# Row norms of a Mamba and attention kernel, computed in two halves of their rows

## The chip, the cores and the metric

The kernel runs on one core of a Trainium2 chip. The metric is the device time of one execution in microseconds. Three runs of the kernel before took 3666.76, 3668.60 and 3671.24 us; their median is 3668.6 us.

A core has engines that each work through their own fixed list of instructions, in order: TensorE (PE, matmuls and transposes; PEld is its weight load), VectorE (DVE), ScalarE (ACT), GpSimd (POOL) and SyncE (SP, which here only issues DMAs). An instruction waits on semaphores for results of other engines, and everything behind it on its engine waits with it. POOL issues some DMAs too, in the same list as its arithmetic.

## The reference, cut to what matters

Eight sequences of 512 tokens with 256 features go through a Mamba layer and then a layer of attention with gated experts and a feed-forward network. Everything is float32.

```python
x = x + _layernorm(mamba(_layernorm(x)))
x = x + _layernorm(moe_layer(_layernorm(x)))

def _layernorm(x, axis=-1, eps=1e-05):
    m = jnp.mean(x, axis=axis, keepdims=True)
    v = jnp.var(x, axis=axis, keepdims=True)
    return (x - m) / jnp.sqrt(v + eps)

def moe_layer(src):
    src = _ln(src + _moe_attn(src), ln1_g, ln1_b)
    return _ln(src + relu(src @ W1 + b1) @ W2 + b2, ln2_g, ln2_b)
```

Each sequence so meets six row norms: before Mamba, after it, before the attention layer, the two inside (`_ln`, with a gain and an offset behind), and one after. Mamba contains a scan over the 512 tokens for 512 channels and 16 states. The attention has 16 heads of width 64; values and outputs pass through 8 experts per head, of which a gate keeps two.

## The kernel before

**Tiling.** A sequence (here "batch" b, 0 to 7) is held either as rows, tokens on 128 partitions, 4 tiles of 128 tokens with 256 features each, or as features on partitions with the 512 tokens along the free dimension. Transposes on PE (`to_features`, L285 to L291) turn one into the other.

**Stages of a batch.** `front(b)` (L305) loads the rows (`xin`), norms them to `xn_m`, transposes (`ps_tr_m`), projects (`ps_in`), runs the convolution on DVE (`xs`) and prepares the step sizes (`ln`, `u`). `mamba(b)` (L500) runs the scan: 32 steps of three DVE instructions each, a product `h<-bt,dtx`, a scan `h<-da,h` and a product `h<-h,ct`, all 128x1024; the two states of a step are summed into `xc` by accumulating DMAs, which POOL issues (L574). Then come the output projection (`ps_out`), the norm of `x`, the residual sum, the norm to `xn`, its transposes (`ps_tr_g`), the gate scores (`ps_sel`) and the gate's selection on DVE (`key`, `hit`, `s`, `top`). Attention goes through 8 pairs of heads (`Pair`, L797): queries and keys `ps_qk`, which are rotated by `sin` and `qk` on DVE and four accumulating DMAs issued by POOL (L841); scores `ps_s`, their maximum `low` (DVE), exponentials (ACT), transposes `ps_pt`, values `ps_v`, weighted by the gate into `ve` (DVE) and added up by three instructions on POOL (L932 to L934) into `v`; the product `ps_o`; the gated `og` (DVE) and the output sums `ps_a`. `feed_forward(b)` (L1026) follows beside the next batch's attention, with the norms of `y` and two of `z`. The last batch's feed-forward network is `last_net` (L1121), in two halves of 256 tokens, whose norms of `y_last` have two row tiles instead of four.

**A norm.** `_Norm.__call__` (L74) is a generator. For each row tile it issues two DVE instructions, the sums (`bn_stats`, into `ln_st`) and their aggregate (`bn_aggr`, mean and variance into `ln_mv`). Then one DVE instruction adds epsilon to the variances of all tiles (`tensor_scalar`, into `ln_rs`), one POOL instruction takes them to the power of -0.5 (L85, in place in `ln_rs`), and for each tile one DVE instruction applies it: subtract the mean, multiply by `ln_rs`. All DVE instructions pass through the wrapper `_Vector`, so they all have line 175 in the profile. There are 51 norms: 45 of four row tiles and 6 of two.

**What sets the order.** The kernel writes out the order of each engine's instructions itself (`manual_schedule`), from a planner (`_Order`, L98). PE's work carries planned durations (`pe`), DVE's too (`_Vector`: 0.02 us, later 0.09 more, and 1.12 ns a column). Attention is the main line; fronts, Mamba layers, feed-forward networks and gates are generators that run beside it. What a generator yields is the planned time until its next part is due, counted from the end of its last DVE instruction in the plan:

```python
        r[0] = max(self.here, self.vec if self.vec > vec else 0.0) + wait
```

A part is put into the order when it is due and the planned DVE has room (`run`, L145); of several that are due, the one of lowest rank goes first. So a yielded number decides which other instructions stand between two parts of a norm in DVE's list, and how early the transposes behind the norm stand in PE's. It makes no engine wait on the chip. In `last_net` the norm's parts are run one after the other with no regard to the yields (`normed`, L1166).

Of the kernel before, what the change touches and what calls it, by code (L numbers as in the profile page):

```python
# [28 lines left out]
ALU = mybir.AluOpType  # L29
# [13 lines left out]
EPS = 1e-5  # L43
# [22 lines left out]
class _Norm:  # L66
# [7 lines left out]
    def __call__(self, out, rows):  # L74

        nc, vector, n = self.nc, self.vector, len(rows)
        st = self.pool.tile([P, n, 6], F32, tag="ln_st", name="ln_st")
        mv = self.pool.tile([P, n, 2], F32, tag="ln_mv", name="ln_mv")
        rs = self.pool.tile([P, n], F32, tag="ln_rs", name="ln_rs")
        for i, r in enumerate(rows):  # L80
            vector.bn_stats(st[:, i, :], r)
            vector.bn_aggr(mv[:, i, :], st[:, i, :])
            yield 0.0
        vector.tensor_scalar(rs, mv[:, :, 1], EPS, None, ALU.add)
        nc.gpsimd.tensor_tensor(rs, rs, self.power[:, :n], ALU.pow)  # L85
        yield 1.5
        for i, r in enumerate(rows):
            vector.tensor_scalar(
                out[:, i, :], r, mv[:, i, 0:1], rs[:, i : i + 1], ALU.subtract, ALU.mult
            )  # L90
            yield 0.1
# [1291 lines left out]
```

## Time and profile before

| What | Value |
|---|---|
| Median of three runs | 3668.6 us |
| Profiled execution | 3673.76 us, its span 3672.0 us |
| Mean granted TensorE clock | 0.970 |
| Powers of 128x4 on POOL | 45, 73.1 us busy, 1624 ns mean |
| Powers of 128x2 on POOL | 6, 4.2 us busy, 698 ns mean |
| Aggregates on DVE | 192, 35.0 us busy, 182 ns mean |
| DVE idle before applications, until a power | 53.5 us, 34 times |
| POOL idle before powers, until the TENSOR_SCALAR of `ln_rs` | 161.2 us, 32 times |

The profile is one execution, slower than the median of the runs by 5.2 us. Its page gives busy times, a chain of waits and groups of instructions; the trace behind it answers for single tiles, stages and instructions. An engine's idle time counts only where the engine, or what waits for it, is on the way to the end. Durations of single instructions include the time in which they were held up once started. Successive DVE instructions overlap by some 0.08 us, so four applications of 0.41 us take 1.38 us.

### The profile page before, as it was taken

How to read it: one execution, taken by the hardware profiler on the slowest of the kernel's cores; microseconds unless marked ns; L12 is line 12 of the kernel's file. 1: busy time of each engine (PE TensorE's matmuls, PEld its weight loads, DVE VectorE, ACT ScalarE, POOL GpSimd, SP SyncE). 2: the span in 40 equal slices, each digit the busy share in tenths (PEclk: the TensorE clock that was granted, in tenths of full speed). 3: DMA queues.
4: the chain of work that ended last, by engine and by line, in shares of the span. 5: the costliest groups of instructions: out<-in, count | busy, mean ns of one | idle time of the engine just before them, and what ended most of it. 6: DMA issues, size and time to landing. Idle time of an engine off the chain costs nothing.

```text
span 3672.0 us, 35171 instructions
## 1 busy us (share of the span) xinstructions
PE 3406.9 (93%) x11250; PEld 1678.2 (46%) x11250; DVE 3048.9 (83%) x3198; ACT 1664.0 (45%) x2866; POOL 1677.5 (46%) x1597
## 2 busy tenths in 40 slices
PE   5768989989899999999999999999999999999997
PEld 3533334444344444444444444445444444446555
DVE  7878898799989898999989998899988999654443
ACT  5624443545543455344644446444553444332332
POOL 1425663354645545354454555355443657232321
PEclk8879999999999999999999999999999999999999
DMA  4927774577866768577755868568765778443430
GB/s 136 198 73 175 179 173 115 150 181 176 196 144 165 176 169 195 124 182 181 197 139 143 203 154 204 146 154 188 183 171 128 181 186 203 118 126 92 115 106 26
DMA packets 282534, 574.06 MB, mean 156 GB/s; under 512 B 37224, under 2 KB 124520, under 8 KB 282096
## 3 DMA queue, kind: packets, MB, share of 16 engines
q1 hardware_dynamic: 201584, 422.88, 40.0%
q0 software_dynamic: 80768, 148.95, 24.3%
q8 instruction: 91, 1.49, 0.2%
q14 instruction: 91, 0.75, 0.1%
HBM read 403.36 MB, written 19.42 MB: 115 GB/s over the span
## 4 chain that ended last, share of the span: by engine, by line
PE 48%; DVE 27%; issue 8%; DMA 7%; ACT 5%; POOL 5%; SPq 0%; DVEq 0%; POOLq 0%; ACTq 0%
PE ps_v L916 14%; DVE h L175 11%; PE ps_a L1000 9%; DMA xc<-h 5%; PE ps_qk L819 5%; PE ps_s L857 4%; PE ps_a L1020 3%; PE ps_o L946 3%; PE ps_pt L892 3%; DVE ve L175 2%; DVE og L175 2%; DVE low L175 2%; DVE xs L175 2%; PE ps_in L347 1%; DVE hit L175 1%
## 5 line engine op out<-in xcount | busy, mean ns | idle before, releaser
L916 PE MATMUL ps_v<-wv,xt 128*128 128x512 f32 x2048 | 945.8, 605 | 20.4 <-DVE y L175 13.3
L932 POOL TENSOR_TENSOR ve<-ve 128x512 f32<-128x512 f32 x256 | 423.6, 1655 | 1148.1 <-DVE ve L175 996.5
L1000 PE MATMUL ps_a<-og,wo 128*128 128x512 f32 x1792 | 847.1, 606 | 28.0 <-DVE og L175 27.7
L872 ACT ACTIVATE p<-ps_s,low 128x512 f32<-128x512 f32 x512 | 347.3, 683 | 723.0 <-DVE low L175 722.6
L574 POOL DMA_DIRECT2D xc<-h x504 | 463.8, 1099 | 382.1 <-DMA xc<-h 170.0
L916 PEld LDWEIGHTS ps_v<-wv,xt 128*128 128x128 f32 x2048 | 385.9, 193 | 536.9 <-issue 481.3
L175 DVE TENSOR_TENSOR_SCAN h<-da,h 128x1024 f32<-128x1024 f32 x228 | 541.2, 2374 | 10.3 <-ACT da L511 0.4
L1000 PEld LDWEIGHTS ps_a<-og,wo 128*128 128x128 f32 x1792 | 326.5, 192 | 440.9 <-issue 371.4
L881 ACT ACTIVATE p<-p,total 128x512 f32<-128x512 f32 x512 | 341.5, 714 | 252.2 <-DVE total L175 251.4
L175 DVE TENSOR_TENSOR og<-o,gb 128x1024 f32<-128x1024 f32 x256 | 320.1, 1271 | 128.8 <-ACT o L952 81.6
L175 DVE TENSOR_TENSOR ve<-ps_v,gv 128x1024 f32<-128x1024 f32 x256 | 311.7, 1218 | 130.0 <-PE ps_v L916 102.7
L898 ACT COPY pt<-ps_pt 128x1024 f32<-128x1024 f32 x256 | 256.9, 1005 | 347.3 <-PE ps_pt L892 345.9
L511 ACT ACTIVATE da<-dt,decay 128x511 f32<-128x511 f32 x512 | 339.8, 714 | 103.9 <-DVE h L175 100.8
L175 DVE TENSOR_TENSOR h<-bt,dtx 128x1024 f32<-128x1024 f32 x228 | 321.2, 1409 | 34.6 <-DMA xc<-h 34.4
L175 DVE TENSOR_TENSOR h<-h,ct 128x1024 f32<-128x1024 f32 x256 | 338.0, 1320 | 3.8
L175 DVE TENSOR_REDUCE low<-ps_s 128x2 f32<-128x1024 f32 x256 | 310.8, 1214 | 26.8 <-PE ps_s L857 26.1
L933 POOL TENSOR_TENSOR ve<-ve 128x256 f32<-128x256 f32 x256 | 318.1, 1243 | 20.1
L841 POOL DMA_DIRECT2D qk<-sin x256 | 204.5, 1209 | 256.7 <-DVE qk L175 128.9
L857 PE MATMUL ps_s<-qk 64*128 64x512 f32 x1024 | 295.0, 650 | 24.3 <-ACT p L872 14.0
L892 PEld LDWEIGHTS ps_pt<-ident,p 128*128 128x128 f32 x2048 | 239.4, 141 | 124.1 <-issue 87.1
L946 PE MATMUL ps_o<-pt,v 128*64 128x512 f32 x1024 | 249.9, 615 | 30.8 <-POOL v L934 16.7
L892 PE MATMUL ps_pt<-ident,p 128*128 128x128 f32 x2048 | 266.8, 274 | 6.4 <-ACT pt L898 2.6
(165 smaller groups left out, 3579.0 us busy)
## 6 DMA issues: line engine op xcount, KB each, us to landing
gb<-go_d SPq DMA_DIRECT2D x512, 256.0 KB, 4.8
xc<-h POOLq DMA_DIRECT2D x504, 256.0 KB, 5.6
wv<-in_wv_dram SPq DMA_DIRECT2D x128, 512.0 KB, 5.9
wo<-in_wo_dram SPq DMA_DIRECT2D x504, 128.0 KB, 4.0
ct<-bc_d SPq DMA_DIRECT2D x64, 512.0 KB, 5.8
bt<-bc_d SPq DMA_DIRECT2D x57, 512.0 KB, 5.6
wqk<-in_wqk_dram SPq DMA_DIRECT2D x64, 256.0 KB, 2.7
qk<-sin POOLq DMA_DIRECT2D x256, 64.0 KB, 4.8
```

What stands on the lines that cost most here:

```text
L175: return getattr(self.engine, name)(*args, **kw)
L511: nc.scalar.activation(das[k % 2][:, j, 1:S], dt[:, m, 1:S], AF.Exp, scale=decay[:, m, g + j : g + j + 1],)
L574: nc.gpsimd.dma_start(out=xc[:, k % NC, :], in_=hs[k][:, j, :], accum_op=ALU.add)
L857: nc.tensor.matmul(ps[:, j, :], lhsT=self.qk[feats, 0, bass.ts(t, P)], rhs=self.qk[feats, 1, :], start=True, stop=True,)
L872: nc.scalar.activation(p[:, j, :], ps[:, j, :], AF.Exp, bias=low[:, j : j + 1], accum_out=total[:, j : j + 1],)
L881: nc.scalar.mul(p[:, j, :], p[:, j, :], total[:, j : j + 1])
L892: nc.tensor.transpose(pp[:, j, bass.ts(i, P)], self.p[t][:, j, bass.ts(i, P)], ident)
L916: nc.tensor.matmul(ps[:, i, :], lhsT=self.xt[:, c, bass.ts(t + i, P)], rhs=self.wv[:, c, :], start=(c == 0), stop=(c == ND - 1),)
L932: nc.gpsimd.tensor_tensor(ve[:, :, 0:4], ve[:, :, 0:4], ve[:, :, 4:8], ALU.add)
L933: nc.gpsimd.tensor_tensor(ve[:, :, 0:2], ve[:, :, 0:2], ve[:, :, 2:4], ALU.add)
L946: nc.tensor.matmul(po[j * HP : j * HP + HP, 0, :], lhsT=self.v[:, j, t, :], rhs=self.pt[:, j, t, :], start=(t == 0), stop=(t == NT - 1),)
L1000: nc.tensor.matmul(pa[:, c, :], lhsT=self.wo[:, i, bass.ts(c, P)], rhs=self.og[q][:, i, :], start=(self.pair == 0 and k == 0), stop=(self. ...
```

## The change

A norm goes through its row tiles in two halves. After the sums and aggregates of a half, its own small `tensor_scalar` and its own power on POOL are issued, so there are two of each per norm, on half the columns. The first half's two instructions stand in front of the second half's sums, in the same part of the generator. The second half's follow its last aggregate. Then 0.6 instead of 1.5 is yielded to the planner before the applications, which are as before. A norm of two row tiles becomes two halves of one tile.

```diff
-        for i, r in enumerate(rows):
-            vector.bn_stats(st[:, i, :], r)
-            vector.bn_aggr(mv[:, i, :], st[:, i, :])
-            yield 0.0
-        vector.tensor_scalar(rs, mv[:, :, 1], EPS, None, ALU.add)
-        nc.gpsimd.tensor_tensor(rs, rs, self.power[:, :n], ALU.pow)
-        yield 1.5
+
+        for at in (slice(0, n // 2), slice(n // 2, n)):
+            for i in range(at.start, at.stop):
+                vector.bn_stats(st[:, i, :], rows[i])
+                vector.bn_aggr(mv[:, i, :], st[:, i, :])
+                yield 0.0
+            vector.tensor_scalar(rs[:, at], mv[:, at, 1], EPS, None, ALU.add)
+            nc.gpsimd.tensor_tensor(rs[:, at], rs[:, at], self.power[:, at], ALU.pow)
+        yield 0.6
         for i, r in enumerate(rows):
             vector.tensor_scalar(
                 out[:, i, :], r, mv[:, i, 0:1], rs[:, i : i + 1], ALU.subtract, ALU.mult
```

## The prediction

> **What bounds the kernel.** I read the page's head first, then the busy times by stage, then what TensorE (PE) waited for, then the reciprocal root itself (the tile `ln_rs`), last single norms in order of time.
>
> ```profile
> span 3672.0 us, 35171 instructions
> PE 3406.9 (93%) x11250; PEld 1678.2 (46%) x11250; DVE 3048.9 (83%) x3198; ACT 1664.0 (45%) x2866; POOL 1677.5 (46%) x1597
> PE 48%; DVE 27%; issue 8%; DMA 7%; ACT 5%; POOL 5%; SPq 0%; DVEq 0%; POOLq 0%; ACTq 0%
> ```
>
> PE is busy for 93% of the span, and the change takes no matmul away: all it can win is part of PE's 265 us of idle time. The busy times by stage (length, PE, PEld, DVE, ACT, POOL, then clock, DMA) say where that lies:
>
> ```profile
> 0.00:222.00 222.00, 136.02 (x630) 96.09 (x630) 177.94 (x185) 109.52 (x180) 56.34 (x78) 0.83 0.66 156
> 860.00:1290.00 430.00, 398.78 (x1258) 186.64 (x1256) 388.97 (x387) 203.84 (x343) 221.13 (x202) 0.97 0.72 170
> 1720.00:2150.00 430.00, 413.51 (x1317) 194.22 (x1316) 385.83 (x403) 205.89 (x351) 215.68 (x198) 0.99 0.68 168
> 3651.00:3672.00 21.00, 6.66 (x31) 5.52 (x29) 13.26 (x36) 0.00 (x0) 2.78 (x4) 0.72 0.07 25
> ```
>
> 86 us of it lie before 222 us (batch 0's Mamba, little else to run), 159 between 222 and 3400, 14 in the last 21, where VectorE (DVE) ends the kernel alone. In the steady stages both PE and DVE are about nine tenths busy. What PE waited for from 222 to 3400 us (total, times, longest):
>
> ```profile
> PE ps_a L1000 <- DVE og L175: 27.7, 9, 6.2
> PE ps_v L916 <- DVE y L175: 13.3, 6, 3.3
> PE ps_tr_g L290 <- DVE xn L175: 4.1, 4, 1.1
> ```
>
> With the answer's other waits that end on DVE this makes some 86 of the 159 us, but only the last row hangs on a norm directly. So a norm costs PE mainly through DVE's own lost time. That is in the tile's view: DVE idle before the applications, until the power came.
>
> ```profile
>   DVE ln_rs L175: 60.5, 22
>   POOL ln_rs L85: 45.2, 25
> ```
>
> In this stretch lie 41 of the 51 norms; 25 made DVE wait, 45.2 us in all.
>
> **One norm, before.** This is a norm with no other DVE work behind its TENSOR_SCALAR (TS, variance plus epsilon): start, length, engine.
>
> ```profile
> 586.46 0.18 DVE L175 BATCH_NORM_AGGREGATE ln_mv<-ln_st 128x2 f32<-128x6 f32 x1
> 586.68 0.17 DVE L175 TENSOR_SCALAR ln_rs<-ln_mv 128x4 f32<-128x4 f32 x1
> 586.93 1.02 POOL L85 TENSOR_TENSOR ln_rs<-ln_rs,minus_half 128x4 f32<-128x4 f32 x1 [1.24 <-DVE ln_rs L175]
> 587.98 1.38 DVE L175 TENSOR_SCALAR x<-x,ln_mv,ln_rs 128x256 f32<-128x256 f32 x4 [1.13 <-POOL ln_rs L85]
> ```
>
> From the last aggregate's end (586.64) to the last application's (589.36) it takes 2.72 us, 1.13 of it waiting.
>
> **What is removed and added.** 45 powers of 128x4 become 90 of 128x2; the 6 of 128x2 (the last batch's half norms) become 12 of 128x1. The two widths cost 1.03 and 0.70 us when alone, so a column is 0.165 us, and 128x1 about 0.53 (an estimate from these two). Each norm gets one TS more, 0.17 us plus its gap: 0.2. The first power starts one TS after the second row's sums and has two rows of sums (4 instructions, about 1.1 us, as from 5.8 to 7.0 us) to finish in. Does it run at its own speed beside sums? No row has it, but GpSimd's adds L933 and L934 often lie beside sums alone and keep 0.73 and 0.46 us. I take the first power of a four-row norm as hidden; if POOL is in other work it comes late and the gain shrinks, to a loss of 0.4 at worst (two powers of 0.70 for one of 1.03). That the change does what it says can be read from the order written for it: application 0 waits for the first power alone, application 2 for the second, and the second TS for no power. A power that waits for its TS holds up what is queued behind it on POOL: the value adds (L932 to L934, for which `ps_o` waits), the `xc` DMAs, the rotation's DMAs. Such waits were 60.5 us in 22 norms above. The first of the two now ends about 1.3 us earlier than the old one, the second 0.2 later, so I charge nothing for it here; it returns among the rivals.
>
> **The second power: row against rule.** It is ready about 0.08 us after the second TS, while applications 0 and 1 may start at once. Side by side, the norm would take 0.2 + 0.21 (gap, TS) + 0.08 + 0.70 + 0.03 + 0.73 (two applications) = 1.95 us, a gain of 0.77. But these rows show POOL and DVE side by side:
>
> ```profile
> 720.65 0.46 POOL L934 TENSOR_TENSOR v<-ve 128x128 f32<-128x128 f32 x1
> 720.67 0.47 DVE L175 TENSOR_SCALAR ln_rs<-ln_mv 128x4 f32<-128x4 f32 x1
> 721.05 1.21 DVE L175 TENSOR_TENSOR h<-bt,dtx 128x1024 f32<-128x1024 f32 x1
> 721.21 1.94 POOL L85 TENSOR_TENSOR ln_rs<-ln_rs,minus_half 128x4 f32<-128x4 f32 x1
> ```
>
> The TS lasted as long as the POOL add beside it (0.47, not 0.17); the power beside `h<-bt,dtx` took 1.94, not 1.03: it ended 0.89 us after that operation. An application beside an add (at 1283.39 us) took 0.87 instead of 0.41. The rule behind it speaks against this change: the Trainium skill, "SBUF — State Buffer", section Who interferes with whom, says that a VectorE tensor_scalar in its two-port mode, or an operation with two SBUF inputs, and a GpSimd operation lock each other out for the whole instruction. By it, application 0 holds the port, then the power, then the other three follow: 0.2 + 0.21 + 0.33 + (0.70 - 0.15, as the row above shows some 0.15 of a power's start under the lock) + 0.03 + 1.06 = 2.4, a gain of about 0.3. Rows and rule agree that the overlap is lost, so I take **0.3**, with 0.77 as the upper end. The section also lets a norm's sums (one input) run beside the power; the adds above show it.
>
> **The path at both ends.** The first norm (4.75 us) is bare: 0.3. Batch 0's two norms after Mamba are where PE sits idle for 13.4 us until `xn`. Before, the planner's 1.5 put `dt<-dt,ln` (1.22 us, two SBUF inputs) behind the first TS, and the power took 1.93: from TS to last application 3.42 us. In the order written with 0.6 it moves behind; 2.0 + 0.2 remain, a gain of 1.2. The second keeps one such operation of two: nothing. The moved operations fall into the 6.8 us in which DVE then waits for `ps_sel`. Start: 1.5. In the last batch five of six half norms are on the path (the second hides under hidden-layer matmuls). Before 1.76 us from sums to end; now 0.2 + 0.21 + 0.33 + 0.38 + 0.03 + 0.41 = 1.56 or, if the short power waits the whole application, nothing won. I take 0.1 each: 0.5.
>
> **The middle.** In the order written for the changed kernel, 22 of these 41 norms have nothing between second TS and applications (19 before). In 4 of them the second power stands behind the rotation's four DMA issues (3.23 us on POOL; 3 norms before, each waiting 4.8). New waits: 18 x 0.6, 4 x (4.8 - 0.7) and some 3 for the others: 30. More TS: 41 x 0.2 = 8. So 38 for 45.2: DVE gets **7 us** back (14 with no lock; minus 8 if the waits don't shrink). PE's idle time ends on DVE a little more than half the time, so I pass on half: 3.5, between 0 and 7.
>
> Not to be read from any row is the new order: with norms declared shorter, transposes, projections and gates of the next batches change places with attention's matmuls. The stages from 1290 to 3010 us, with their own orders, are idle for 14 to 17 us each: 1.5 us of scatter a stage, some 5 over the kernel, either sign; the two stages with 31 to 32 could move more.
>
> **Sum.** 1.5 + 0.5 + 3.5 = 5.5 us from the profiled execution's 3673.8 (span 3672.0 and 1.8 around it): 3668.3. That execution lies 5.2 above the runs' median, 3668.6, so the median becomes **3663**.
>
> **Rivals.**
> - *No lock in practice*: powers slip between applications, 0.77 a norm; DVE gets 14 us back and PE most of it, with start and tail 4 more: 3652. For it: POOL sometimes wins at once. Against: the 0.87 row.
> - *A wash*: the added TS eat the shorter waits, PE keeps its idle time: 3668. For it: only 4.1 us of PE's waits hang on norms.
> - *Slower*: POOL's fixed order. The second power sits behind rotation issues or adds (2.5 us a set), while the planner, told 0.6, puts `ps_tr_g` and `ps_tr_m` earlier in PE's fixed order; PE stalls with all attention behind it. Before, two norms behind the issues cost PE 2 us each (1916, 2769 us). Should the 14 transposes of 7 batches stall 1 us each, 14 minus 2 won: 3681. It decides from an average stall of 0.4 us. Against: planned time behind the second TS (0.6 + four applications at 0.4 and 0.1 = 2.6) is still above the 2.2 worked out.
>
> **Chances.** Forecast (gain 2 to 10) 0.47, no lock 0.16, wash 0.16, slower 0.21. 0.2%, about what a measurement can tell, is 7.3 us. Faster: the no-lock case and under half of the forecast's, 0.37; slower 0.22; same 0.41. The range goes from the no-lock case to the slow one's edge: 3651 to 3680.
>
> **What would show it.** The added TS at 0.17; first powers at 0.70 beside sums; second powers 0.8 to 1.1 or applications stretched to about 1.0 beside them (lock) or neither (no lock); DVE's wait for powers near 30 us; the first scores' start 1 to 2 us earlier. Wrong: PE waits for `xn` or `xn_m` above 10 us after 222, or stages at 1290 to 3010 whose idle time moves by more than 5 us.

## The result, and the profile after

The changed kernel takes 3710.0 us (median of four runs, 3705.3 to 3716.7), the kernel before 3669.9 beside it: a ratio of **1.0105** (95% interval 1.0090 to 1.0121). It is slower by 1%, where 3663 us, faster by 0.15%, was forecast. First the head of its page and its chain of waits, as shown of before:

```profile
span 3708.7 us, 35263 instructions
...
PE 3420.2 (92%) x11250; PEld 1680.6 (45%) x11250; DVE 3076.3 (83%) x3249; ACT 1664.0 (45%) x2868; POOL 1696.9 (46%) x1648
...
PE 46%; DVE 30%; issue 8%; DMA 7%; POOL 4%; ACT 4%; SPq 0%; DVEq 0%; POOLq 0%; ACTq 0%
```

The span grew by 36.7 us. PE, with the same 11250 matmuls, is busy for 13.3 us more, at a mean granted clock of 0.967 against 0.970 in these two executions. Runs of the kernel before alone range from 0.966 to 0.973, so two profiles don't tell how much of this part belongs to the change. The rest, 23.4 us, is more idle time of PE (265.1 to 288.5). DVE is busy for 27.4 us more. By stages (columns as before; a stage of steady work is longer now, the two shown here are 435 and 430 us):

```profile
0.00:222.00 222.00, 141.29 (x632) 101.00 (x633) 177.72 (x188) 110.96 (x181) 57.36 (x82) 0.81 0.66 156
867.00:1302.00 435.00, 397.62 (x1239) 185.50 (x1238) 392.30 (x383) 206.23 (x346) 219.65 (x203) 0.96 0.71 169
1736.00:2166.00 430.00, 412.57 (x1308) 192.17 (x1306) 395.28 (x412) 206.64 (x352) 221.19 (x206) 0.98 0.71 171
```

PE's idle time is length less busy: 80.7 us at the start (86 before), 37.4 in the stage that had 31.2, 17.4 in the one that had 16.5. The start gained, the steady batches lost. Where the loss adds up shows in when `ps_o` of a batch's first pair begins, later than before by

| Batch | 0 | 1 | 2 | 3 | 4 | 5 | 6 | 7 |
|---|---|---|---|---|---|---|---|---|
| us | -1.8 | 2.6 | 12.4 | 20.6 | 28.6 | 28.7 | 38.3 | 35.6 |

that is, by 4 to 10 us in most batches, not in one place. What PE waited for from 222 to 3435 us (total, times, longest):

```profile
PE ps_a L1002 <- DVE og L177: 40.1, 17, 5.9
...
PE ps_x L337 <- ACT xs L406: 12.4, 5, 3.1
PE ps_v L918 <- DVE y L177: 10.1, 5, 3.0
...
PE ps_tr_g L292 <- DVE xn L177: 3.5, 6, 1.5
```

The waits that end on a norm (`ps_tr_g`, and `ps_tr_m` at 1.7) stayed small. Those for gates (`ps_a`, 27.7 before) and for Mamba's Silu (`ps_x`, 2.3 before) grew by 22.5 us together; neither hangs on a norm directly. The norms themselves did what the change says. The tile `ln_rs` from 222 to 3440 us, its engines' idle time before it:

```profile
  DVE ln_rs L177: 124.8, 45
  POOL ln_rs L87: 22.5, 18
```

DVE's wait for powers halved (45.2 us before), while POOL's wait for the TSs doubled (60.5 before). And one bare norm, batch 0's first after Mamba (start, length, engine, line):

```profile
209.33 0.17 DVE L177 TENSOR_SCALAR ln_rs<-ln_mv 128x2 f32<-128x2 f32 x1
209.41 0.42 DVE L177 BATCH_NORM_STATS2 ln_st<-x 128x6 f32<-128x256 f32 x1
209.58 0.71 POOL L87 TENSOR_TENSOR ln_rs<-ln_rs,minus_half 128x2 f32<-128x2 f32 x1 [23.11 <-DVE ln_rs L177]
...
210.60 0.17 DVE L177 TENSOR_SCALAR ln_rs<-ln_mv 128x2 f32<-128x2 f32 x1
210.68 0.73 DVE L177 TENSOR_SCALAR x<-x,ln_mv,ln_rs 128x256 f32<-128x256 f32 x2
210.85 0.78 POOL L87 TENSOR_TENSOR ln_rs<-ln_rs,minus_half 128x2 f32<-128x2 f32 x1 [0.56 <-DVE ln_rs L177]
211.67 0.73 DVE L177 TENSOR_SCALAR x<-x,ln_mv,ln_rs 128x256 f32<-128x256 f32 x2 [0.26 <-POOL ln_rs L87]
```

The first power lies beside the third row's sums at its own speed, the second beside two applications, both nearly at theirs. From the first sum (208.12) to the last application (212.40) this takes 4.28 us; the bare norm of before took 4.94 (584.42 to 589.36). So a bare norm is faster. With what stands between their parts, 36 of the 51 norms are shorter than before and 15 longer, and the kernel is slower.

### The profile page after: what moved, and what is told of

Read it like the earlier page. It is cut to its first block, busy times and chain, and to the rows that moved or that the text cites. A ratio compares the mean times of both kernels' runs of the same rounds, so it can differ in the third digit from the quotient of the medians.

```text
span 3708.7 us, 35263 instructions
## 1 busy us (share of the span) xinstructions
PE 3420.2 (92%) x11250; PEld 1680.6 (45%) x11250; DVE 3076.3 (83%) x3249; ACT 1664.0 (45%) x2868; POOL 1696.9 (46%) x1648
## 4 chain that ended last, share of the span: by engine, by line
PE 46%; DVE 30%; issue 8%; DMA 7%; POOL 4%; ACT 4%; SPq 0%; DVEq 0%; POOLq 0%; ACTq 0%
PE ps_v L918 13%; DVE h L177 11%; PE ps_a L1002 8%; PE ps_qk L821 5%; DMA xc<-h 4%; PE ps_s L859 4%; PE ps_a L1022 3%; PE ps_o L948 3%; DVE ve L177 3%; PE ps_pt L894 2%; DVE low L177 2%; DVE og L177 2%; PE ps_in L349 2%; DMA gb<-go_d 2%; DVE hit L177 1%
## 5 line engine op out<-in xcount | busy, mean ns | idle before, releaser
L934 POOL TENSOR_TENSOR ve<-ve 128x512 f32<-128x512 f32 x256 | 415.0, 1621 | 1069.1 <-DVE ve L177 925.6
L177 DVE TENSOR_TENSOR h<-bt,dtx 128x1024 f32<-128x1024 f32 x228 | 329.1, 1443 | 42.9 <-DMA xc<-h 42.9
```

Source lines behind the costliest of these rows:

```text
L177: return getattr(self.engine, name)(*args, **kw)
L934: nc.gpsimd.tensor_tensor(ve[:, :, 0:4], ve[:, :, 0:4], ve[:, :, 4:8], ALU.add)
```

## The experiments

Two theories at first. **Halves cost**: the added TSs, the powers held up and holding up on POOL and DVE make the norms worse for the whole, though one alone is shorter. **Order costs**: the halves gain, but the planner, told of one more DVE instruction and of 0.6 us for 1.5, writes another order for every engine, and that order is worse. An order is compared by the least number of instructions that must be moved to get it from the order of before (those that touch `ln_rs` are left out of the count): for the change 618 of the 2957 counted in DVE's list and 302 of the 6805 in PE's.

**Norm and order crossed.** The halves in exactly the order of before: both TSs go past the planner, which is then charged for the one TS it knew.

```diff
         for i, r in enumerate(rows):
+            if i == k:
+                add(slice(0, k))
+                power(slice(0, k))
             vector.bn_stats(st[:, i, :], r)
...
-        vector.tensor_scalar(rs, mv[:, :, 1], EPS, None, ALU.add)
-        nc.gpsimd.tensor_tensor(rs, rs, self.power[:, :n], ALU.pow)
+        add(slice(k, n))
+        power(slice(k, n))
+        vector.order.vector(0.02 + vector.order.more + 1.12e-3 * n)
         yield 1.5
```

> The norm in two halves, but with the planned time of a whole norm and its 1.5, so that every engine's list stands in the order of before, with the added TENSOR_SCALARs and powers put in. If the new ORDER makes the changed kernel slow: 3655 to 3670 us (0.996 to 1.000 of before), DVE waits for powers about 25 us, PE idle time as before. If the HALVES themselves do (13 us more TENSOR_SCALAR time, 11 us of applications held up by the second power, two powers in POOL's list): 3695 to 3710.

The whole norm in the changed kernel's order: the reverse, one TS and one power, and the planner charged for two TSs and told 0.6 (a few of SP's DMA issues stand one place off).

> Whole norms, one TENSOR_SCALAR and one power each as before, but with the changed kernel's planned times and its 0.6, so in the changed kernel's order. If the ORDER makes it slow: 3705 to 3725 us (1.010 to 1.015), as slow as the changed kernel or slower, since the waits for the whole power come back. If the HALVES do: 3665 to 3680.

The whole norm with 0.6 alone, and the halves with 1.5 alone, each one line (`yield 1.5` to `yield 0.6`, and back):

> Whole norms with only the number changed, 0.6 for 1.5: a third order, unlike both. ORDER: anywhere from 3665 to 3715, and the place of its loss is where its own order differs; if applications planned too early are the cause as such, 3695 to 3715. HALVES: 3665 to 3680.

> The changed kernel with 1.5 in place of 0.6: halves, and a fourth order. If the number 0.6 is the cause: 3655 to 3675. If any order other than the tuned one costs: 3680 to 3715. HALVES: 3695 to 3715 whatever the order.

Measured: 0.9974 (0.9960 to 0.9988), 1.0166 (1.0149 to 1.0184), 1.0214 (1.0197 to 1.0230) and 1.0036 (1.0023 to 1.0049). At a fixed order the halves win twice: 0.26% in the old one, 0.6% in the new one (1.0105 against 1.0166). The order costs 1.3% with halves (0.9974 to 1.0105) and 1.7% without. The first theory is refuted. The tile `ln_rs` over the same stretch, halves in the old order, then the whole norm in the new one:

```profile
  DVE ln_rs L82: 82.6, 39
  POOL ln_rs L81: 11.0, 14
```

```profile
  DVE ln_rs L87: 97.7, 24
  POOL ln_rs L88: 50.5, 25
```

Of these four kernels the halves in the old order wait least for powers (11.0 us) and are the one that beats before. Short waits for powers are not enough for that: the halves with 1.5 wait 13.0 us and are slower than before.

**Is it the short wait, or any other order?** Four more orders: the kernel before with an unrelated wait nudged (`after(2.0, scaled)` to 2.05, the softmax's scaling; 398 DVE and 180 PE instructions moved by the count above, two thirds of the change's; the expectation's 910 and 932 are counted otherwise), the whole norm told 1.0 and 2.2, the halves told 2.2.

> The kernel before, its norms untouched; only the wait that the planner is told between a softmax's exponentials and its scaling is 2.05 us instead of 2.0. That moves about as many VectorE instructions as the change does (910 of 2957, against 932), none of them meant. Theory A (the order costs because norms are planned shorter than they take: the direction decides): within 0.2% of before, ratio 0.998 to 1.002. Theory B (the order of before was picked among many, and any other costs): about what the halves with the old wait lost against the halves in the old order, 0.6%: ratio 1.003 to 1.010.

> The whole norm with the planner told 1.0 us instead of 1.5 (0.6 gave 1.0214). Fewer instructions move: 267 on VectorE, 90 on TensorE. Theory A: between the two, by the share of the way some 1.008 to 1.013. Theory B: cost follows the number of moved instructions and not the wait, 1.001 to 1.006.

> The whole norm with the planner told 2.2 us, longer than a power takes alone; 917 VectorE and 1286 TensorE instructions move. Theory A: not slower than before, 0.995 to 1.002, with VectorE's wait for powers clearly under 53 us. Theory B: slower, 1.003 to 1.012, though VectorE waits less.

> The halves with the planner told 2.2 us (0.6 gave 1.0105, 1.5 gave 1.0036). Theory A: the series goes on falling, 0.996 to 1.002. Theory B: no trend, anywhere from 1.002 to 1.010.

Measured: 1.0056 (1.0038 to 1.0073), 1.0067 (1.0047 to 1.0086), 1.0054 (1.0034 to 1.0074), 1.0011 (1.0001 to 1.0022). A nudge of 0.05 us in a wait that has nothing to do with norms costs 0.56%, more than the forecast had for the whole change. This is what another order can cost that nobody meant. The halves still fell with a longer wait (1.0105, 1.0036, 1.0011), which looked like a cost of the short wait besides. The same two waits beside another nudge (`after(1.8, scaled)`) put that to the test:

> The changed kernel (halves, planner told 0.6) with the softmax's wait told as 1.8 instead of 2.0, which moves another 546 of VectorE's instructions. The question of these four: is the cost of 0.6 over 2.2 one of the wait itself, or did one order draw badly? With the softmax at 2.0 the halves lost 0.9% by 0.6 against 2.2 (1.0105 to 1.0011), the whole norm 1.6% (1.0214 to 1.0054). Theory A+B (any other order costs some 0.5%, and the short wait its own cost besides): 1.008 to 1.014, and slower than the halves with 2.2 of this set by 0.5% or more. Theory B alone: 1.002 to 1.008, with no settled sign against the halves with 2.2.

> The halves with 2.2, and the softmax's wait 1.8. Theory A+B: 1.000 to 1.006, faster than both whole norms of this set. Theory B alone: 1.002 to 1.008.

> The whole norm with 0.6, and the softmax's wait 1.8. Theory A+B: 1.016 to 1.024, the slowest of this set. Theory B alone: 1.004 to 1.010.

> The whole norm with 2.2, and the softmax's wait 1.8. Theory A+B: 1.003 to 1.009, as with the softmax at 2.0. Theory B alone: the same.

Measured: 1.0112 (1.0092 to 1.0132), 1.0163 (1.0146 to 1.0180), 1.0137 (1.0122 to 1.0152), 1.0089 (1.0072 to 1.0106). The trend broke: the halves with 2.2 are now the slowest of the set, where they had been nearly level with before. Which order a small number happens to give weighs more than the wait itself. In the twelve runs so far, every order but the old one was slower than before, by 0.1 to 2.1%.

**One stall taken out.** Batch 4's `ps_x` in PE's list, beside batch 2's attention, first before, then after:

```profile
1354.18 3.70 PE L1000 MATMUL ps_a<-og,wo 128*128 128x512 f32 x8
1357.81 3.62 PE L335 MATMUL ps_x<-xs,w_x 128*33 128x512 f32 x8
```

```profile
1355.22 3.65 PE L948 MATMUL ps_o<-pt,v 128*64 128x512 f32 x16
1361.93 6.54 PE L337 MATMUL ps_x<-xs,w_x 128*33 128x512 f32 x8 [3.06 <-ACT xs L406]
```

After, `ps_x` stands right behind `ps_o` and waits 3.06 us for a Silu, in this and the three following batches alike (4 to 7; the expectation below calls them 3 to 6). The wait is not its whole price: the eight matmuls behind it took 6.54 us for 3.62, at a granted clock of 0.55 against 1.00 before, and 4.93 to 5.32 us in the other three. With the planner told 4.0 for that Silu (`yield free(2.2)` to `yield free(4.0)`, L414) it moves behind `ps_v` in three of them.

> The changed kernel with one wait told longer: the Silu of Mamba's convolved rows (ACT), before the matmuls ps_x, as 4.0 us instead of 2.2. In the changed kernel's order ps_x stands right behind ps_o in batches 3 to 6 and TensorE waits 3.06 us for that Silu each time; before, ps_x stood behind ps_a and did not wait. With 4.0 only 52 of 6805 TensorE and 31 of 2957 VectorE instructions move, and ps_x stands behind ps_v in three of these four batches. Theory R (the new order's cost is stalls that come back in every batch, and a stall taken out of TensorE's order comes out of the time): ps_x waits 3 to 4 us in all instead of 12.4, time 6 to 10 us below the changed kernel's, ratio 1.007 to 1.009. Theory S (the time is set elsewhere, the idle time only changes its place): the wait at ps_x goes, others grow, ratio 1.010 to 1.012.

Measured: 1.0116 (1.0099 to 1.0133), no better than the changed kernel (1.0090 to 1.0121). PE's waits between 1180 and 3285 us, of the changed kernel and then of this one:

```profile
PE ps_x L337 <- ACT xs L406: 12.2, 4, 3.1
...
PE ps_o L948 <- ACT pt L900: 6.4, 4, 2.7
...
PE ps_v L918 <- ACT p L874: 1.1, 2, 0.7
```

```profile
PE ps_o L948 <- ACT pt L900: 16.8, 8, 3.2
...
PE ps_v L918 <- ACT p L874: 7.5, 4, 4.0
...
PE ps_x L337 <- ACT xs L406: 3.1, 1, 3.1
```

9 us of waiting at `ps_x` went, and 17 us came at two places of attention that wait for ACT's part of the softmax. They stand in the three batches in which `ps_x` moved, 26 to 56 us behind it. Theory S of this run holds: a stall that PE is spared there is waited for later. One of the two waits that had grown most was so not the cause by itself; the other, `ps_a` (12.4 us more), was not tried.

**Which norms.** The short wait told to half of the norms only, by an argument to `_Norm.__call__`; the three around Mamba (its input, its output, the one before selection) or the feed-forward's three; first in whole norms, then in halves, the others at 1.5.

```diff
-    def __call__(self, out, rows):
+    def __call__(self, out, rows, wait=1.5):
...
-        yield 1.5
+        yield wait
...
-            yield from norm(xn, [xin[:, t, :] for t in range(NT)])
+            yield from norm(xn, [xin[:, t, :] for t in range(NT)], 0.6)
```

> The kernel before, whole norms, with 0.6 told only for the three norms of a batch around Mamba (its input, its output, the one before selection), 1.5 for the feed-forward's three. All six at 0.6 gave 1.0214. Theory Q (one group's new place carries the loss): 1.016 or more here and under 1.005 for the other group, or the other way round. Theory B (each reordering of this extent costs by itself; 673 VectorE and 276 TensorE instructions move): 1.004 to 1.016 in both, and the two need not add up to 1.0214.

> The kernel before, whole norms, with 0.6 told only for the feed-forward's three norms; 539 VectorE and 260 TensorE instructions move. Theory Q: under 1.005 if the group around Mamba carries the loss, 1.016 or more if this one does. Theory B: 1.004 to 1.016.

> The changed kernel (halves) with 0.6 told only for the three norms around Mamba, 1.5 for the feed-forward's three. All at 0.6: 1.0105; all at 1.5: 1.0036. In whole norms the Mamba group alone gave 1.015, the other 1.0032. If the group's place decides, in halves too: 1.008 to 1.012. If each order draws anew: anywhere from 1.001 to 1.016, without regard to the group.

> The changed kernel with 0.6 told only for the feed-forward's three norms, 1.5 for the Mamba group. If the group's place decides: 1.001 to 1.005, at least 0.4% under the other run of this pair. If each order draws anew: anywhere from 1.001 to 1.016.

Measured, whole norms: Mamba group 1.0150 (1.0133 to 1.0168), feed-forward 1.0032 (1.0019 to 1.0045). Halves: 1.0062 (1.0047 to 1.0077) and 1.0016 (1.0005 to 1.0027). Neither theory is met to the letter in whole norms: one run fell just short of 1.016, the other lies under 1.004. In halves one run was below 1.008, and both lie where a fresh draw of the order could have put them. But the sign is the same twice, by 1.2% and by 0.5%. The nearest reading is that the norms around Mamba, whose applications stand ahead of the transposes and projections of a whole batch, carry more of the loss than those of the feed-forward. Two pairs among orders that scatter by a per cent suggest it; they do not prove it.

The kernel before, the change and the first twelve runs in one table; "softmax" is the planner's wait before the scaling, moved is DVE's count against the order of before, idle is PE's in the profiled execution:

| Norm | Told | Softmax | Moved | PE idle, us | Ratio |
|---|---|---|---|---|---|
| whole (before) | 1.5 | 2.0 | 0 | 265 | 1 |
| halves, old order | 1.5 | 2.0 | 0 | 257 | 0.9974 |
| whole | 1.5 | 2.05 | 398 | 276 | 1.0056 |
| whole | 1.0 | 2.0 | 271 | 284 | 1.0067 |
| whole | 2.2 | 2.0 | 726 | 270 | 1.0054 |
| whole | 0.6 | 2.0 | 740 | 317 | 1.0214 |
| whole, the change's order | 0.6 | 2.0 | 618 | 309 | 1.0166 |
| whole | 2.2 | 1.8 | 776 | 288 | 1.0089 |
| whole | 0.6 | 1.8 | 650 | 303 | 1.0137 |
| halves (the change) | 0.6 | 2.0 | 618 | 289 | 1.0105 |
| halves | 1.5 | 2.0 | 460 | 263 | 1.0036 |
| halves | 2.2 | 2.0 | 620 | 266 | 1.0011 |
| halves | 0.6 | 1.8 | 741 | 297 | 1.0112 |
| halves | 2.2 | 1.8 | 741 | 303 | 1.0163 |

## Why the prediction was wrong

**The step that failed** is the one left nearly unpriced: "Not to be read from any row is the new order", put at "some 5 over the kernel, either sign", from the spread of idle time between four neighbouring stages of one kernel. Those stages all have the order that was there, so their spread says nothing of another. Measured at fixed norm, the new order cost 48 us with halves (0.9974 to 1.0105 of 3670) and 61 without. And it was not "either sign": in none of the table's twelve rows with another order, nor in the last five runs, was the time below that of before. The order of before is a good one among those that this planner writes; that could have been asked of the lists of instructions (618 and 302 moved) but not priced from the profile of before. Without this term the sum has the right sign and order of size: in the old order the halves gained 0.26%, some 9.5 us, where 5.5 were forecast. Its parts did not come out as forecast, as follows.

**The start** was forecast at 1.5 us and gained 1.6 (batch 0's `ps_tr_g` from 219.5 to 217.9 us). That the sum fits is luck. The first norm gained 0.74 for 0.3, but nothing of it was left at the norm after Mamba, which began 0.9 us later than before (208.12 for 207.22). The two norms there gained 1.6 and 0.8, where 1.2 and nothing were forecast.

**The lock.** The gain of a bare norm was taken as 0.3, by the rows with a POOL add and by the Trainium skill, "SBUF — State Buffer", section Who interferes with whom, which has a `tensor_scalar` in its two-port mode and a GpSimd operation shut each other out; "no lock" was the upper end, 0.77. Measured 0.66: the second power took 0.78 us beside the applications, against 0.71 beside sums, and the applications kept their 0.73 for two. In this trace 15 powers lay beside applications alone and took 0.75 to 0.83 us, 26 beside sums alone and took 0.69 to 0.71. This pair of instructions does not lock; the measurement decides. An application beside a POOL add was held (the prediction's 0.87 us); why it is not beside this power, no run shows, nor whether the application meets the page's condition, the two-port mode. What the row of before showed of a two-input operation stayed true. Start, length, of batch 0's second norm:

```profile
216.25 1.22 DVE L177 TENSOR_TENSOR dt<-dt,ln 128x1024 f32<-128x1024 f32 x1
216.42 1.73 POOL L87 TENSOR_TENSOR ln_rs<-ln_rs,minus_half 128x2 f32<-128x2 f32 x1 [0.52 <-DVE ln_rs L177]
```

The 128x2 power, 0.71 alone, took 1.73 beside `dt<-dt,ln` and ended 0.68 after it.

**DVE in the middle.** Its wait for powers was forecast to fall from 45.2 to 30 us and fell to 22.5. But the instructions around it grew more than the 8 us of added TSs: over the kernel the TSs went from 11.0 to 24.0 us in sum and the applications from 92.1 to 102.9, held up beside POOL's value adds (38 of them by more than 0.1 us, 22 before, each beside such an add). That is the order's doing: the applications take 101.9 with whole norms in the new order and 92.0 with halves in the old one. (The first run's expectation puts them down to the second power; this refutes it.) Wait, TSs and applications together are 156.6 us before (53.5, 11.0, 92.1) and 152.3 after (25.4, 24.0, 102.9), ends included: DVE got 4 us back, and 0.4 in the stretch for which 7 were forecast (135.2 to 134.7). In the old order the same halves give 128.7 (13.6, 23.1, 92.0), 28 us back, and the kernel passed on 7 of them by the spans (3672.0 to 3664.8): a quarter, not the half that I had taken. The two misses work against each other.

**The tail** was forecast to gain 0.5. Each of its norms did shorten (2.99 to 2.65 us from sums to end in one), but the last batch's `ps_a` matmuls ahead of them took 10.59 us for 8.90 at a lower granted clock (0.96 against 1.00 in that stage), as they did with halves in the old order. From the issue of the last output DMA to the end it took 5.1 us for 3.5, which no run explains. The stretch as a whole lost 2 us.

**The rivals.** "Slower" came closest in sign, but by another mechanism: it wanted PE to stall at `ps_tr_g` and `ps_tr_m`, and these waits are 5.2 us in all after 222 us. What the prediction named as the sign of its failure, a stage between 1290 and 3010 us whose idle time moves by more than 5 us, did show in one of the four (13.9 to 19.9 us, in stretches of about the same work), before and after:

```profile
1290.00:1720.00 430.00, 416.09 (x1327) 194.50 (x1324) 396.07 (x413) 210.02 (x355) 217.83 (x201) 0.99 0.72 172
```

```profile
1302.00:1736.00 434.00, 414.06 (x1312) 193.13 (x1312) 386.58 (x407) 204.06 (x349) 217.10 (x206) 0.98 0.69 165
```

The two stages ahead of these, which were said to move more, did so by 6 to 7 us each (31.2 to 37.4 in the second).

**What stays open** is why one order is worse than another. The waits tell where PE stood, and taking one away moved them. That the loss lies in no one stall is shown for the stall that was tried, not for the others; that the norms around Mamba carry more of it is suggested.

## What to carry to other kernels

Where a planner writes the order of every engine from planned times, no local edit is local: here 0.05 us in an unrelated wait cost 0.56%, more than the edit's own gain of 0.26%. Before judging an edit, run it once in the old order (charge the planner what it was charged, issue the new instructions past it), and keep that version if the edit wins there; here it is the only one that beats before. And price a reorder by nudging something unrelated, not by the spread between stages of one order.

## What was not expected of the hardware

A 128x2 power on POOL and 128x256 applications on DVE ran side by side (0.78 and 0.73 us, against 0.71 and 0.73), while the same power beside a 128x1024 operation with two tensor inputs was held for all but its last 0.68 us. And an order's price is paid partly in idle time and partly in slower matmuls. Behind each of the four waits of 3.06 us at `ps_x`, its eight matmuls took 4.93 to 6.54 us for 3.62, at granted clocks of 0.73 to 0.55. Over a whole kernel this can be told only from all runs of an order, since the kernel before alone ranges from 0.966 to 0.973: the halves with the short wait in the feed-forward alone had 0.968 to 0.972 (PE busy for 3405 us in the profiled one), the halves with 2.2 and 1.8 had 0.965 to 0.967 (3432 us, for the same 11250 matmuls).
